# Last layer's scans: one exponential per four states, products added before TensorE sums them

## The chip, the cores and the metric

The kernel runs on one core of a Trainium2 chip. The time is the device time of one execution in microseconds. Before the change the median of three runs is 20188.83 us (20176.15 to 20194.05).

The core has five engines that run side by side, each through its own queue in order: TensorE (PE; its weight loads are listed apart as PEld), VectorE (DVE), ScalarE (ACT), GpSimd (POOL), and SyncE (SP), which here issues the DMAs. Semaphores order work between them.

## The reference, cut to what matters

Four layers in a row work on an image tensor of 8 x 48 x 48 x 96. Each is `x = x + ss2d(groupnorm(x))`. The block `ss2d` projects to 192 channels, applies a 3 x 3 depthwise convolution and a silu, and then runs four state-space scans over the 2304 pixels (by rows, by columns, and both reversed), each with 16 states per channel. A layer norm, a gate and an output projection close it.

The last layer writes its scan as cumulative sums:

```
dt = softplus(dt @ dt_proj_w + dt_proj_b)
A = -exp(A_log)
log_dA = einsum('bld,dn->bldn', dt, A)
dB_u = einsum('bld,bln->bldn', dt, B_mat) * u[..., None]
decay = exp(cumsum(log_dA, axis=1))
h = decay * cumsum(dB_u / (decay + 1e-12), axis=1)
y = einsum('bldn,bln->bld', h, C_mat)
```

The decay falls so fast along a sequence that after some pixels it is zero in float32, and `h` with it. So only a first part of each sequence can give anything.

## The kernel before, in words

The eight images are taken as four pairs. Per pair the 2 x 192 channels fill three tiles of 128 partitions: the first 128 channels of each image, and the last 64 of both together. A group is one tile (`t`), one pixel order (`ph`, rows or columns) and one direction (`d`): twelve groups per pair and layer.

In layers 0 to 2 a group is cut into `Chunk`s of 768 pixels. The last layer is handled by the class `Edge`: of each sequence only the first `EDGE` = 192 pixels are computed. A check at the very end looks whether the decay was zero there everywhere; if not, the last layer would be run again in full. In the executions here it is not run again.

An edge has 16 states, taken as four units of `QUAD` = 4 states. A unit's arrays are 128 x 4 x 192 (768 columns). For a unit:

- `load` (L930 on) has SP fetch the four rows of C, spread over the partitions, into `cb` (nine buffers).
- `decay` (L949) writes the four decays into `da` (four buffers): four ScalarE exponentials of 192 columns, each with the rate of its state as scale (L953). Its input `dl` is the running sum of delta, which `prepare` and `sum_up` (L911) have made.
- `spread` (L958) makes `rq` = 1/(decay + eps) with two activations (L960, L961) in one of three buffers of tag `bb`, and has TensorE spread the rows of B into PSUM (`b`, L678).
- `scan` (L970) multiplies on VectorE (L973, L974), runs four running sums of 192 columns into `rq` (L976), and has GpSimd multiply `cb` by the decay (L980) and by the sums (L981).
- `add_up` (L983) adds the 16 products of an edge in PSUM (`acc`, one buffer): one matmul with the identity per state (L988). `collect` then adds `acc` into `y` on VectorE (L1010).

`prepare` (L583 on) makes delta and delta x u of an edge: a small projection (L614), activations for the softplus (L622 to L628), four TensorE sums in two column halves (L634), a copy (L652) and a product (L642, L645). `dl` and `du` have two buffers.

The function `run` writes the units in program order. In step k it readies unit k+1 (`get_ready`: loads for three units ahead, decay two ahead, spread of the next), scans unit k, and sums unit k-2 (`LAG`). Beside each unit in the last layer up to ten steps of side work are issued: the prologue of the next pair (norm, projection L411 and L420, convolution L314, later projections L472) and the epilogue of the pair before (L1031 to L1140, in 16 blocks, with silu and its table loads at L270 and L271). `prepare`, prologue and epilogue share two PSUM banks (`ps`).

A planner in the framework decides when each instruction goes to its engine's queue: with priority by program order, with its own estimates of durations, and as buffers become free. `keep_order(*marks[:2])` pins the written order from the start to the last layer's first unit. In the last layer the order within the queues is thus the planner's.

Of the kernel before, what the change touches and what calls it, by code (L numbers as in the profile page):

```python
# [41 lines left out]
AF = mybir.ActivationFunctionType  # L42
ALU = mybir.AluOpType
# [6 lines left out]
P = 128  # L50
# [3 lines left out]
NS = 16  # L54
# [8 lines left out]
EDGE = 4 * W  # L63
QUAD = 4
# [39 lines left out]
def ss2d_layers_kernel(ctx: ExitStack, tc: tile.TileContext, x_in, consts, weights, out):  # L104
    nc = tc.nc
# [25 lines left out]
    ident = cst[:, 0:P]  # L131
# [54 lines left out]
    class Layer:  # L186


        def __init__(self, l):
            self.l = l  # L190
            self.rank = r = RANKS[l]
            self.nx = nx(r)
            cols, n = weight_columns(r)
            wt = wpool.tile([P, n], F32, name=f"w_{l}", tag="w")
            nc.sync.dma_start(wt, weights[l])
            part = {k: wt[:, a:b] for k, (a, b) in cols.items()}
            self.inw = part["inw"][0:DM]
            self.xp = part["xp"].rearrange("p (t f m) -> p t f m", t=2, f=2)
            self.dtw = part["dtw"].rearrange("p (k d) -> p k d", k=4)
            self.outw = part["outw"].rearrange("p (t c) -> p t c", t=2)  # L200
            self.par = part["par"].rearrange("p (t c) -> p t c", t=2)
            self.diag = None
# [56 lines left out]
    layers = {}  # L259
# [440 lines left out]
    class Chunk:  # L700
# [71 lines left out]
        def decay(self, n):  # L772

            if not self.pooled(n):
                self.exp(n, apool.tile([P, SCAN], F32, name="da", tag="da"))
# [26 lines left out]
        def scan(self, n):  # L802
            m = self.m
            way = (lambda z: z) if self.d == 0 else (lambda z: z[:, ::-1])
            carries = self.group["carry"]
            start = 0.0 if self.first else carries[:, n : n + 1]
            da, c = self.da.pop(n), self.cb[n][:, :m]
            b = self.b.pop(n)[:, :m]
            if not self.pooled(n):
                nc.vector.tensor_mul(b, self.du[n % 2], b)  # L810
            if self.l < NLAYER - 1:

                h = b if self.pooled(n) else da
                nc.vector.tensor_tensor_scan(way(h), way(da), way(b), start, ALU.mult, ALU.add)  # L814
            else:

                h = self.rq.pop(n)
                nc.vector.tensor_mul(b, h, b)
                nc.vector.tensor_tensor_scan(
                    way(h), ones.to_broadcast([P, m]), way(b), start, ALU.mult, ALU.add  # L820
                )
                nc.gpsimd.tensor_mul(c, c, da)
            nc.gpsimd.tensor_mul(c, c, h)  # L823
            if not self.last:
                end = m - 1 if self.d == 0 else 0
                late_act.append((carries[:, n : n + 1], h[:, end : end + 1]))
# [33 lines left out]
        def add_up(self, n):  # L860

            if n == 1:
                self.begin_sum()
            if n == 0:
                return
            pair = n - 1 - (n - 1) % 2
            a = n - 1 - pair
            for g in range(2):
                c = self.halves(self.cb[pair + g][:, : self.m])
                nc.tensor.matmul(  # L870
                    self.acc[64 * g : 64 * g + 64, a, : self.m // 2], twin, c[:, a, :],
                    start=False, stop=(pair + 2 == NS and not self.turns),
                )
                if a == 1:
                    del self.cb[pair + g]
            if n == NS and not self.turns:
                late_sums.append(self.collect)
# [18 lines left out]
    class Edge:  # L896


        def __init__(self, l, p, t, ph, d):
            self.l, self.p, self.t, self.ph, self.d = l, p, t, ph, d  # L900
            self.c0, self.m = 0 if d == 0 else L - EDGE, EDGE
            self.at = slice(self.c0, self.c0 + EDGE)
            self.first, self.last = ph == d == 0, ph == d == 1
            self.batches = range(2) if t == 2 else (t,)
            self.brow = self.acc = self.dts = None
            self.ready = False
            self.cb, self.da, self.rq, self.b = {}, {}, {}, {}

        def sum_up(self):
            f = self.dl[0] if self.d == 0 else self.dl[0][:, ::-1]  # L910
# [37 lines left out]

        def decay(self, i):  # L949
            self.da[i] = da = self.quad(apool.tile([P, SCAN], F32, name="da", tag="da"))  # L950
            for j in range(QUAD):
                n = (self.ph + 2 * self.d) * NS + QUAD * i + j
                nc.scalar.activation(  # L953
                    da[:, j, :], self.dl[0], AF.Exp,
                    scale=layers[self.l].a[:, int(self.t == 2), n : n + 1],
                )

        def spread(self, i):  # L958
            self.rq[i] = rq = self.quad(bbpool.tile([P, SCAN], F32, name="rq", tag="bb"))
# [9 lines left out]

        def scan(self, i):  # L970
            way = (lambda z: z) if self.d == 0 else (lambda z: z[:, ::-1])
            b, h, c = self.b.pop(i), self.rq.pop(i), self.cb[i]
            nc.vector.tensor_mul(b, self.du[0].unsqueeze(1).to_broadcast([P, QUAD, EDGE]), b)  # L973
            nc.vector.tensor_mul(b, h, b)  # L974
            for j in range(QUAD):
                nc.vector.tensor_tensor_scan(  # L976
                    way(h[:, j, :]), ones.to_broadcast([P, EDGE]), way(b[:, j, :]), 0.0,
                    ALU.mult, ALU.add,
                )
            nc.gpsimd.tensor_mul(c, c, self.da.pop(i))  # L980
            nc.gpsimd.tensor_mul(c, c, h)  # L981

        def add_up(self, i):  # L983
            if i == 0:
                self.acc = pacc.tile([P, 2 * BANK], F32, name="acc", tag="acc")
            c = self.cb.pop(i)
            for j in range(QUAD):
                nc.tensor.matmul(  # L988
                    self.acc[:, :EDGE], ident, c[:, j, :],
                    start=(i == j == 0), stop=(QUAD * i + j == NS - 1),  # L990
                )
            if QUAD * i + QUAD == NS:
                late_sums.append(self.collect)
# [430 lines left out]
```

## Time and profile before

| | |
|---|---|
| median of the runs | 20188.83 us |
| profiled execution | 20200.44 us |
| its span | 20198.6 us |
| busy: PE, DVE, ACT, POOL | 16790.8, 17667.0, 16224.6, 17769.4 us |
| last layer's units (first L953 to last L988) | 18289 to 19961 us |
| last epilogue, alone | 19963 us to the end |

A row of the profile's groups gives line, engine, operation, written and read tiles, shapes and count, then busy time in us and the mean ns of one, then the idle time of the engine just before the group, with what ended it. A 128*128 before a matmul's shapes is rows by columns of the weights; a float32 matmul shows as two records. In the table of windows, each pair of figures is an engine's busy time and its instruction count; PEclk is the share of TensorE's full clock that was granted. The chain of waits is followed back from the last instruction, at each step to what released it.

### The profile page before, as it was taken

Reading aid. Unit: us, or ns where it says so; the run is one execution under the profiler, and the core shown is the slowest. Engines: PE = TensorE matmul, PEld = TensorE weight load, DVE = VectorE, ACT = ScalarE, POOL = GpSimd, SP = SyncE. Lnnn points to the kernel's source line nnn. Section 1 sums busy time; section 2 is a strip of 40 time slices with the busy share of each in tenths; the row PEclk is TensorE's granted clock in tenths of the full one; section 3 lists DMA queues with packets and bytes.
Section 4 is the critical chain, followed back from the end, with each engine's and each line's share of the span. In section 5 each row is a group of like instructions: output and inputs, shape, how many; then the busy total and the mean of one; then the engine's idle time right before and its main releaser. Section 6 shows DMA issues by size and latency. Waiting matters only on the chain.

```text
span 20198.6 us, 314848 instructions
## 1 busy us (share of the span) xinstructions
PE 16790.8 (83%) x92962; PEld 7792.6 (39%) x92962; DVE 17667.0 (87%) x14161; ACT 16224.6 (80%) x30014; POOL 17769.4 (88%) x10121
## 2 busy tenths in 40 slices
PE   7888887887888888888887888888888887888886
PEld 3333333333333333333333333333333333334565
DVE  6999998998999999999999999999999999996553
ACT  6777887887887887887887887877877887887786
POOL 6999999999999999999999999999999999995442
PEclk9998998998998998998998999998999998999997
DMA  5888888888888888888888888888888888884221
GB/s 157 231 224 223 226 222 221 227 223 220 225 226 224 224 231 224 223 228 223 225 228 223 223 225 226 223 226 221 221 224 222 222 225 221 220 222 117 79 74 50
DMA packets 2021150, 4200.80 MB, mean 208 GB/s; under 512 B 375920, under 2 KB 789360, under 8 KB 2017904
## 3 DMA queue, kind: packets, MB, share of 16 engines
q1 hardware_dynamic: 2019440, 4180.55, 79.2%
q8 instruction: 762, 12.48, 0.3%
q14 instruction: 948, 7.77, 0.2%
HBM read 4026.64 MB, written 152.27 MB: 207 GB/s over the span
## 4 chain that ended last, share of the span: by engine, by line
PE 21%; ACT 17%; DVE 14%; DMA 10%; issue 9%; POOL 3%; SPq 2%; DVEq 0%; POOLq 0%; ACTq 0%
DVE da L814 7%; PE acc L870 5%; PE ps L634 4%; DMA bb<-xd 4%; DVE b L810 4%; DMA cb<-xd 4%; ACT b L780 3%; ACT dl L589 3%; PE ps L314 2%; PE b L678 2%; ACT du L589 2%; POOL cb L823 2%; DVE bb L814 2%; ACT da L780 2%; SPq L740 1%
## 5 line engine op out<-in xcount | busy, mean ns | idle before, releaser
L823 POOL TENSOR_TENSOR cb<-cb,da 128x768 f32<-128x768 f32 x4320 | 7835.9, 1819 | 749.3 <-issue 253.1
L870 PE MATMUL acc<-cb,twin 128*64 128x384 f32 x27648 | 7200.8, 539 | 721.3 <-POOL cb L823 704.5
L814 DVE TENSOR_TENSOR_SCAN da<-da,carry,b 128x768 f32<-128x768 f32 x2880 | 5223.2, 1814 | 176.0 <-DVE b L810 0.9
L757 POOL TENSOR_TENSOR bb<-bb,du 128x768 f32<-128x768 f32 x2592 | 4716.9, 1820 | 222.2 <-DMA bb<-xd 125.6
L823 POOL TENSOR_TENSOR cb<-cb,bb 128x768 f32<-128x768 f32 x2592 | 4706.8, 1816 | 100.2 <-DVE bb L814 50.7
L810 DVE TENSOR_TENSOR b<-du,b 128x768 f32<-128x768 f32 x4320 | 4085.6, 946 | 690.2 <-PE b L678 604.2
L678 PE MATMUL b<-brow,pick 96*64 96x512 bf16 (+2 forms) x18816 | 2852.5, 353 | 1886.2 <-DVE da L814 1528.4
L780 ACT ACTIVATE da<-dl,a 128x768 f32<-128x768 f32 x4320 | 4011.3, 930 | 213.5 <-POOL cb L823 183.0
L870 PEld LDWEIGHTS acc<-cb,twin 128*64 128x64 f32 x27648 | 2452.5, 149 | 2998.4 <-POOL cb L823 1333.5
L814 DVE TENSOR_TENSOR_SCAN bb<-b,carry,bb 128x768 f32<-128x768 f32 x1728 | 3109.6, 1800 | 106.0 <-ACT b L780 35.6
L780 ACT ACTIVATE b<-dl,a 128x768 f32<-128x768 f32 x2592 | 2335.3, 901 | 623.2 <-DVE da L814 598.4
L678 PEld LDWEIGHTS <-pick 96*64 96x64 bf16 x18816 | 1077.9, 115 | 4164.4 <-DVE da L814 2717.6
L814 DVE TENSOR_TENSOR_SCAN da<-da,b 128x768 f32<-128x768 f32 x1440 | 2525.3, 1754 | 87.4 <-DVE b L810 1.4
L314 PE MATMUL ps<-pad,diag 128*64 128x480 f32 (+1 forms) x8640 | 2339.7, 567 | 34.6 <-ACT du L589 24.4
L589 ACT COPY dl<-ps 64x384 f32<-64x384 f32 x3456 | 1632.6, 472 | 697.9 <-PE ps L634 659.6
L589 ACT COPY du<-ps 64x384 f32<-64x384 f32 x3456 | 1633.5, 473 | 200.7 <-DVE ps L645 109.8
L634 PE MATMUL ps<-du,cst 128*64 128x384 f32 (+1 forms) x7296 | 1704.5, 506 | 76.5 <-ACT du L628 65.6
L814 DVE TENSOR_TENSOR_SCAN bb<-b,bb 128x768 f32<-128x768 f32 x864 | 1502.1, 1739 | 145.5 <-ACT b L780 92.2
L634 PE MATMUL ps<-dl,cst 128*64 128x384 f32 (+1 forms) x7296 | 1485.2, 483 | 0.0
L614 PE MATMUL ps<-dts,w 6*128 6x384 f32 (+5 forms) x2432 | 961.4, 605 | 205.0 <-DMA dts<-xd 105.4
L622 ACT ACTIVATE du<-ps,w 128x384 f32<-128x384 f32 (+1 forms) x912 | 519.9, 570 | 714.6 <-PE ps L614 701.0
L314 PEld LDWEIGHTS ps<-pad,diag 128*64 128x64 f32 x8640 | 751.8, 139 | 885.0 <-issue 729.6
(144 smaller groups left out, 19166.4 us busy)
## 6 DMA issues: line engine op xcount, KB each, us to landing
cb<-xd SPq DMA_DIRECT2D x13952, 192.0 KB
bb<-xd SPq DMA_DIRECT2D x5184, 192.0 KB
brow<-xb SPq DMA_DIRECT2D x864, 72.0 KB
ey<-yd SPq DMA_DIRECT2D x256, 216.0 KB
cb<-xd SPq DMA_DIRECT2D x128, 384.0 KB
yd<-y SPq DMA_DIRECT2D x216, 192.0 KB
ex<-xs SPq DMA_DIRECT2D x256, 108.0 KB
xb<-parts SPq DMA_DIRECT2D x96, 216.0 KB
```

Of the source, the lines that this page charges most:

```text
L314: nc.tensor.matmul(ps[half, :m], ly.diag[:, int(t == 2), j, half], pad[:, r0 + dy : r0 + dy + nr, dx : dx + W], start=(j == 0), stop=(j == 8),
L589: nc.scalar.copy(z[64 * h : 64 * h + 64, g, at], v[64 * g : 64 * g + 64])
L614: nc.tensor.matmul(o[:, :m], ly.dtw[q0 : q0 + r, k, chans], dts[q0 : q0 + r, at], start=True, stop=True,)
L622: nc.scalar.activation(e, v, AF.Abs, bias=bias)
L634: nc.tensor.matmul(v[half], ident[:, half], z1, start=(i == 0), stop=(i == 3))
L678: nc.tensor.matmul(o[64 * h : 64 * h + 64], pick[:, b, n : n + 1].to_broadcast([2 * NR, 64]), rows, start=True, stop=True,)
L757: nc.gpsimd.tensor_mul(b, b, self.du[n % 2])
L780: nc.scalar.activation(da, self.dl[n % 2], AF.Exp, scale=layers[self.l].a2[:, int(self.t == 2), n % 2, k, i : i + 1],)
L810: nc.vector.tensor_mul(b, self.du[n % 2], b)
L814: nc.vector.tensor_tensor_scan(way(h), way(da), way(b), start, ALU.mult, ALU.add)
L823: nc.gpsimd.tensor_mul(c, c, h)
L870: nc.tensor.matmul(self.acc[64 * g : 64 * g + 64, a, : self.m // 2], twin, c[:, a, :], start=False, stop=(pair + 2 == NS and not self.turns),)
```

## The change

Three edits, all in `Edge`:

1. `decay`: one GpSimd product of `dl` (repeated for four states) and the four rates (repeated over 192 pixels) into `da`, then one ScalarE exponential of all 768 columns in place. The four scaled exponentials go.
2. `scan`: the tile `rq`, which holds the running sums, is kept in `self.h` for later.
3. `add_up`: VectorE adds the four products of the unit over the states (`tensor_reduce` over a rearranged view with a step of 192 columns) into the first 192 columns of the kept `rq` tile, and TensorE adds this one array into `acc`, in two matmuls of 64 columns of the identity instead of four of 128.

```diff
         def decay(self, i):
             self.da[i] = da = self.quad(apool.tile([P, SCAN], F32, name="da", tag="da"))
-            for j in range(QUAD):
-                n = (self.ph + 2 * self.d) * NS + QUAD * i + j
-                nc.scalar.activation(
-                    da[:, j, :], self.dl[0], AF.Exp,
-                    scale=layers[self.l].a[:, int(self.t == 2), n : n + 1],
-                )
+            n = (self.ph + 2 * self.d) * NS + QUAD * i
+            a = layers[self.l].a[:, int(self.t == 2), n : n + QUAD]
+            nc.gpsimd.tensor_mul(
+                da, self.dl[0].unsqueeze(1).to_broadcast([P, QUAD, EDGE]),
+                a.unsqueeze(2).to_broadcast([P, QUAD, EDGE]),
+            )
+            nc.scalar.activation(da, da, AF.Exp)
...
         def scan(self, i):
             way = (lambda z: z) if self.d == 0 else (lambda z: z[:, ::-1])
-            b, h, c = self.b.pop(i), self.rq.pop(i), self.cb[i]
+            b, c = self.b.pop(i), self.cb[i]
+            self.h[i] = h = self.rq.pop(i)
...
         def add_up(self, i):
             if i == 0:
                 self.acc = pacc.tile([P, 2 * BANK], F32, name="acc", tag="acc")
-            c = self.cb.pop(i)
-            for j in range(QUAD):
+            c, z = self.cb.pop(i), self.h.pop(i)[:, 0, :]
+            nc.vector.tensor_reduce(
+                z, c.rearrange("p n m -> p m n"), mybir.AxisListType.X, ALU.add
+            )
+            for g in range(2):
+                half = slice(64 * g, 64 * g + 64)
                 nc.tensor.matmul(
-                    self.acc[:, :EDGE], ident, c[:, j, :],
-                    start=(i == j == 0), stop=(QUAD * i + j == NS - 1),
+                    self.acc[half, :EDGE], ident[:, half], z,
+                    start=(i == 0), stop=(QUAD * i + QUAD == NS),
                 )
```

More of the change, by code (lines that the diff above doesn't have):

```diff
@@ L906, in __init__ @@
             self.ready = False
-            self.cb, self.da, self.rq, self.b = {}, {}, {}, {}
+            self.cb, self.da, self.rq, self.b, self.h = {}, {}, {}, {}, {}
         def sum_up(self):
```

## The prediction

> **What bounds the kernel now.** I first read the page's 40 slices, to find where the changed code runs, because it runs in the last layer only.
>
> ```profile
> PE   7888887887888888888887888888888887888886
> PEld 3333333333333333333333333333333333334565
> DVE  6999998998999999999999999999999999996553
> ACT  6777887887887887887887887877877887887786
> POOL 6999999999999999999999999999999999995442
> ```
>
> For 36 slices GpSimd and VectorE are full; in the last four they fall to about half while TensorE and ScalarE stay at 8. The first quad product (L980) starts at 18,300 us and the last (L981) at 19,955: a stage of 1,673 us from the first exponential, 12 edges x 4 units for each of four pairs, 192 units of 8.7 us. From 19,963 only the last epilogue runs (235 us, without these lines); before 18,290 nothing changes. Next, the engines' busy time in windows cut at the pairs' first units, and then at the end of the third epilogue:
>
> ```profile
> core 0: us, PE busy (x) PEld busy (x) DVE busy (x) ACT busy (x) POOL busy (x), PEclk, DMA share, GB/s
> 18300.00:18723.00 423.00, 372.25 (x2490) 237.03 (x2490) 223.13 (x384) 338.12 (x637) 178.34 (x111) 0.95 0.31 88
> 18723.00:19153.00 430.00, 379.79 (x2653) 252.83 (x2654) 223.94 (x381) 340.51 (x641) 178.05 (x111) 0.93 0.27 77
> 19153.00:19579.00 426.00, 379.00 (x2662) 251.50 (x2660) 221.15 (x375) 340.34 (x641) 177.77 (x107) 0.93 0.27 75
> 19579.00:19824.00 245.00, 184.62 (x1416) 153.59 (x1412) 114.74 (x197) 196.03 (x359) 85.91 (x48) 0.86 0.26 71
> 19824.00:19963.00 139.00, 93.19 (x552) 71.87 (x552) 94.88 (x168) 96.23 (x195) 85.76 (x48) 0.76 0.22 65
> ```
>
> In three pairs PE is busy 0.88 to 0.89, ACT 0.80, DVE 0.52, POOL 0.42. The fourth pair has no prologue to carry. Its first 245 us hold an epilogue of 16 blocks, which alone takes 235 us, so that stretch is paced by the epilogue's own chain. Its last 139 us have no side work: about 25 units at 5 to 6 us. Then the groups of the stage, kept apart by shape:
>
> ```profile
> L976 DVE TENSOR_TENSOR_SCAN rq<-ones,b 128x192 f32<-128x192 f32 x768 | 364.9, 534 | 12.7
> L988 PE MATMUL acc<-cb,cst 128*128 128x192 f32 x1536 | 352.7, 372 | 72.3 <-POOL cb L981 64.2 <-DVE y L1010 6.4 <-ACT y L887 1.3
> L981 POOL TENSOR_TENSOR cb<-cb,rq 128x768 f32<-128x768 f32 x192 | 347.9, 1812 | 499.6 <-DVE rq L976 456.5 <-PE ps L411 17.8 <-ACT eo L1140 8.1
> L980 POOL TENSOR_TENSOR cb<-cb,da 128x768 f32<-128x768 f32 x192 | 347.1, 1813 | 417.2 <-ACT da L953 399.2 <-PE acc L988 10.1 <-PE ps L314 6.1
> L953 ACT ACTIVATE da<-dl,a 128x192 f32<-128x192 f32 x767 | 293.5, 443 | 29.5 <-DVE dl L911 29.0
> ```
>
> The sum's matmuls are the largest TensorE group, and GpSimd's idle 917 us in front of its two products is waiting, not work. Last, the chain of waits in the stage:
>
> ```profile
> by line: PE ps L314 17.6%; PE acc L988 11.0%; DVE rq L976 4.9%; POOL cb L981 4.5%; issue 4.5%; ACT da L953 3.7%; PE ps L1031 3.2%; PE ps L634 2.8%; PE ps L1032 2.6%; PE b L678 2.4%; PE ps L1135 2.1%; POOL cb L980 2.1%; ACT L270 2.1%; PE ps
> ```
>
> Summed by engine, PE holds 928 of 1,673 us of it and ACT 340. So TensorE's in-order queue is the nearest bound, fed through ScalarE; the change takes work from both.
>
> **What the Trainium skill says.** "ScalarE: Activation LUTs", What ACT_TABLE_LOAD costs: 186 ns + 0.833 N, and some 93 ns for each pointer operand. For 192 columns with a pointer scale that is 439 ns, for 768 without one 826; the trace has 440 (L953) and 834 (L961). "GPSIMD Engine Reference", Performance versus the Vector engine: two inputs cost about 2.6 cycles an element, estimated 1,664 ns for 768 before dispatch; the trace has 1,812. "VectorE: DVE Perf Modes", perf-mode tier table: tensor_reduce runs at one element per cycle only. The trace agrees: L231 reads 128 elements in 262 ns, L154 reads 48, strided, in 202. "TensorE: Matmul & The Clock Gate", Part 1: idle gaps lower the clock. The windows agree: 0.95 granted at 0.88 busy, 0.76 at 0.67.
>
> **The change, part by part, per unit.**
>
> ScalarE loses four exponentials. They occupy 292.9 us for 758, overlaps counted once: 1.55 us per unit. It gains one like L961, 0.83. Saved: 0.71 us, 136 us over 192 units.
>
> TensorE loses four 128-column products of 192 columns, eight records: 352.7/192 = 1.84 us. It gains two 64-column halves, four records. The nearest row is L634 (128*64, 128x192, 752 records busy 86.3 us: 0.115 each), so 0.46. Saved: 1.38 us, 265 us in all. Even at L988's 0.23 a record it would be 0.92, still half.
>
> GpSimd gains one product of 768 with two broadcast inputs. No row has a stride-0 input; L980, L981 and L757 give 1.81, which I take. Below, were a repeated operand free of the read port, a single-input loop would be an estimated 1 us by the same page; above, half more (2.7) by its pitfalls table, which names long strides that are absent here. Per pair POOL goes from 178 to 265 us of some 410: room. In the last 139 us it goes from 86 to some 130: no room.
>
> VectorE gains a reduce of 768 to 192. From L231's slope and offset (128/0.96 + 135 ns) it is 0.935; taken 0.95. Its step of 768 bytes has no row here, so the upper end is twice that. DVE per pair: 223 to 269 us.
>
> New waits: an exponential now waits for GpSimd, whose queue holds the product behind L980 and L981 of earlier units, L981 being the one that waits for scans (456 us). Whoever waits for that exponential (L960, L980) waits along. The reduce stands in VectorE's queue behind a POOL result; behind it stand the next L973, L974 and scans. DMA loads and SP's order do not change; the cb buffers come free sooner, after the reduce, at no gain since no large wait names them.
>
> The costliest new hold is the buffer. The reduce writes into rq, of which there are three. Before, rq was free when L981 ended; now it is held to the end of the matmuls. Taking the n-th instruction of each line as unit n, rq's first activation to L981's end is 13.0 us on average, to the end of L988 22.9; three buffers at 8.7 us a unit allow 26.1. It fits on average; in the convolution quarters, where L988 runs up to 17 us after L981, it is at the limit.
>
> **The sum on the chain.** L988: 11.0% of 1,673 = 184 us, scaled 0.46/1.84, is 46: -138. L953: 3.7% = 62, 40 units, at 0.83 is 33: -29. Where the chain comes to that exponential from delta's running sum (25 waits on L911), the GpSimd product is put between: +45. L981's 75 us are 41 visits, each followed by a reduce: +41. That is -81. Clock: other TensorE work on the chain, 928 - 294 - 184 = 450 us, loses some 4% as PE empties: +20. The last 25 units, at POOL's limit: +13. So -48 with the order as it is. The order is planned anew, though: were the three pairs as full of TensorE work as now (0.89), each would be (372 - 66)/0.89 = 344 us instead of 425, some -240 in all. I take a fifth of the way between, since two PSUM banks for all side work and the epilogue's own chain stay: -48 - 38 = -86. The profiled execution took 20,200.4 us (span 20,198.6, 1.8 around it), so 20,114; the runs' median stands 11.6 below it, so about 20,103 there.
>
> **Rivals.** First, a denser plan: TensorE's 265 us are mostly given back, 19,930 to 20,040 us. For it: PE at 0.89. Against: much of the chain is epilogue and convolution, untouched. Second, no gain: GpSimd's product and the reduce, in series between delta and the sum, cost what the matmuls give, 20,148 to 20,230. For it: the last 25 units already run at 5 to 6 us, and each needs 5.4 us of POOL. Third, slower: the rq ring. If L988 goes on 13 us behind L981 in the convolution quarters, a unit's hold is 14.3 (activation to L981) + 4 (GpSimd's fuller queue) + 1.2 (reduce) + 13 + 0.6 = 33 us; a third is 11 us against 9.8, over some 108 units +140, to 20,330. It decides once the hold passes three times the present period. Against it: L988 lags because TensorE is overfull, which the change relieves. That the change does not act is excluded: L953, L980 and L988 are its lines and run 192 units.
>
> **How the numbers follow.** My forecast, 20,040 to 20,148: 0.48, and within it 20,103. Denser plan 0.20, no gain 0.13, ring 0.19. A change under 0.2% (40 us) can't be told from none here: faster 0.68, same 0.13, slower 0.19. From 19,970 (a third of the dense case below) to 20,250 (most of the ring above) holds eight in ten; the unknown costs of product and reduce, at their upper ends 0.9 us each on the 25 and 41 chain visits (+59), lie inside.
>
> **What would show it.** Right: L988 with 768 records of 64 columns near 90 us; one exponential per unit of 0.83; a GpSimd row at 1.81; a reduce at 0.95; pairs one to three near 400 us, PE at 0.76; the last stretch a little longer. Wrong: ACT's first rq activation waiting for TensorE's sum (the ring), a reduce far over 1 us, L973 idle behind the reduce, or PE still above 0.85.

## The result, and the profile after

The change makes the kernel slower: 20396.8 us median (20382.12 to 20410.47), against 20194.05 (20176.15 to 20211.87) for the kernel before on the same chip. The ratio is 1.0102, with a 95% interval of 1.0088 to 1.0116. One thousandth of the time is 20.2 us; all ratios below are turned into us with that, so this one is +206. Every kernel was compared with runs of the kernel before on its own chip.

In the profiled execution the span is 20380.3 us. The last epilogue alone takes 237 us (235 before). The whole difference lies in the 192 units of the last layer: from the start of their first scan to the end of their last, 1,862 us against 1,656, so +206. (What stands ahead of the first scan was 22 us shorter in this execution, so the two spans differ by only 182.) These are the page's 40 slices after the change:

```profile
PE   7887887887888888888888888888888888877775
PEld 3333333333333433433433333433433433334444
DVE  6999999999999999999999999999999999996553
ACT  6777887887887878887878878878878878876665
POOL 6999999999999999999999999999999999995543
```

TensorE and ScalarE have dropped from 8 to 7 and 6 in the last slices, as the change meant them to. VectorE and GpSimd have not risen to full. No engine has become so busy that its load alone would explain the loss, and yet the time is longer. Next, the engines' busy time in windows cut at the pairs' first units, at the end of the third epilogue and at the last unit:

```profile
core 0: us, PE busy (x) PEld busy (x) DVE busy (x) ACT busy (x) POOL busy (x), PEclk, DMA share, GB/s
18285.00:18773.00 488.00, 365.66 (x2286) 221.72 (x2286) 288.62 (x434) 321.64 (x506) 247.54 (x160) 0.80 0.25 74
18773.00:19252.00 479.00, 369.10 (x2474) 227.18 (x2476) 288.32 (x436) 320.57 (x503) 246.81 (x159) 0.81 0.23 69
19252.00:19719.00 467.00, 362.30 (x2464) 225.68 (x2464) 282.15 (x421) 318.25 (x497) 244.78 (x154) 0.83 0.24 69
19719.00:20000.00 281.00, 181.27 (x1385) 146.62 (x1384) 145.98 (x219) 198.80 (x307) 120.81 (x74) 0.77 0.21 62
20000.00:20143.00 143.00, 54.89 (x369) 29.86 (x370) 123.49 (x181) 69.00 (x102) 106.68 (x64) 0.54 0.17 53
```

The pairs take 488, 479, 467 and 424 us, against 423, 430, 426 and 384. TensorE is busy 0.75 of the first pair, ScalarE 0.66, VectorE 0.59, GpSimd 0.51. The loss is spread over all four pairs; the last stretch, where GpSimd was to be tight, adds only some 4 us of it. The granted clock fell from 0.95 to about 0.81. The groups of the stage, kept apart by shape:

```profile
L978 DVE TENSOR_TENSOR_SCAN rq<-ones,b 128x192 f32<-128x192 f32 x764 | 362.0, 533 | 3.3
L994 PE MATMUL acc<-rq,cst 128*64 128x192 f32 x768 | 142.1, 410 | 157.9 <-DVE rq L989 150.2 <-ACT da L957 4.2 <-DVE y L1016 1.9
L983 POOL TENSOR_TENSOR cb<-cb,rq 128x768 f32<-128x768 f32 x192 | 347.9, 1813 | 479.7 <-DVE rq L978 402.6 <-ACT rq L961 20.8 <-ACT eo L1146 8.5
L982 POOL TENSOR_TENSOR cb<-cb,da 128x768 f32<-128x768 f32 x192 | 345.3, 1814 | 79.4 <-ACT da L957 79.1
L957 ACT ACTIVATE da<-da 128x768 f32<-128x768 f32 x188 | 157.3, 838 | 136.6 <-POOL da L953 136.1
L953 POOL TENSOR_TENSOR da<-dl,a 128x768 f32<-128x768 f32 x188 | 270.7, 1465 | 292.9 <-DVE dl L911 278.2 <-DMA cb<-xd 10.9 <-ACT rq L961 2.1
L989 DVE TENSOR_REDUCE rq<-cb 128x192 f32<-128x768 f32 x192 | 285.7, 1488 | 241.4 <-POOL cb L983 241.0 <-DMA brow<-xb 0.2
```

The work that left is gone: the sum's matmuls are busy 142 us instead of 353, the exponentials 157 instead of 294. The three new instructions have something in common: each is preceded by a long idle time of its own engine, and each names another engine as what ended it. The waits of the stage put that beside each other (engine, line and what it waited for: us in total, times, longest us). Of the kernel before:

```profile
POOL cb L980 <- ACT da L953: 399.2, 100, 27.8
DVE b L974 <- ACT rq L961: 173.0, 63, 10.1
PE acc L988 <- POOL cb L981: 64.2, 54, 2.7
ACT da L953 <- DVE dl L911: 29.0, 25, 3.1
```

And of the changed kernel:

```profile
POOL da L953 <- DVE dl L911: 278.2, 37, 31.6
DVE rq L989 <- POOL cb L983: 233.9, 128, 7.7
DVE b L976 <- ACT rq L962: 147.3, 64, 7.8
PE acc L994 <- DVE rq L989: 143.6, 72, 4.8
ACT da L957 <- POOL da L953: 136.1, 91, 6.0
ACT rq L961 <- PE acc L994: 36.7, 22, 3.9
```

Three waits are new and large: VectorE for GpSimd's products (234 us), GpSimd for delta's running sum (278), ScalarE for GpSimd's new product (136). The last line, the `rq` ring of the third rival, is small. The chain of waits in the stage:

```profile
by line: issue 10.1%; PE ps L314 6.7%; POOL cb L983 6.4%; DVE rq L978 5.3%; POOL cb L982 4.8%; POOL da L953 4.7%; DVE rq L989 3.1%; DVE b L976 2.2%; PE ps L1141 1.8%; PE ps L1037 1.7%; PE ps L1142 1.6%; PE ps L1140 1.5%; PE ps L1038 1.3%; A
```

The sum's matmuls have left its first places, and so has most of TensorE: 397 of 1,853 us (18,290 to 20,143), where it was 928 of 1,673. GpSimd (297) and VectorE (254) have taken its place.

### The profile page after: what moved, and what is told of

It is laid out like the page before. It is cut to its first block, busy times and chain, and to the rows that moved or that the text cites. A ratio compares the mean times of both kernels' runs of the same rounds, so it can differ in the third digit from the quotient of the medians.

```text
span 20380.3 us, 313007 instructions
## 1 busy us (share of the span) xinstructions
PE 16716.7 (82%) x92194; PEld 7667.9 (38%) x92194; DVE 17921.1 (88%) x14353; ACT 16147.2 (79%) x29458; POOL 18041.2 (89%) x10313
## 5 line engine op out<-in xcount | busy, mean ns | idle before, releaser
L314 PE MATMUL ps<-pad,diag 128*64 128x480 f32 (+1 forms) x8640 | 2334.9, 569 | 41.3 <-ACT du L589 24.7
L314 PEld LDWEIGHTS ps<-pad,diag 128*64 128x64 f32 x8640 | 756.6, 140 | 896.2 <-issue 732.1
```

The lines of the kernel that those rows point to most:

```text
L314: nc.tensor.matmul(ps[half, :m], ly.diag[:, int(t == 2), j, half], pad[:, r0 + dy : r0 + dy + nr, dx : dx + W], start=(j == 0), stop=(j == 8),
```

## The experiments

The theory after the result: TensorE and ScalarE were busy and on the chain, but no bound, so the work taken from them is worth nothing; the two new hand-overs, GpSimd to VectorE and VectorE to GpSimd to ScalarE, hold the heads of in-order queues, and that costs the 206 us. The rivals were the `rq` ring, the strided reduce (longer than forecast) and the lower clock. As a second measure beside the ratios: in every run's profile, the stretch from the first scan of the stage to the last differs from the kernel before's by the same amount within 25 us.

### The two halves apart

e1 has edit 1 alone (product on GpSimd, one exponential; `scan` and `add_up` as before):

```diff
-            for j in range(QUAD):
...
-                nc.scalar.activation(
...
+            nc.gpsimd.tensor_mul(
+                da, self.dl[0].unsqueeze(1).to_broadcast([P, QUAD, EDGE]),
+                a.unsqueeze(2).to_broadcast([P, QUAD, EDGE]),
+            )
+            nc.scalar.activation(da, da, AF.Exp)
```

> Only the first edit: one GpSimd product and one exponential per unit; the four matmuls per unit stay. In-order theory (the product stands at the head of GpSimd's queue until delta's running sum is there, and the two products of earlier units stand behind it): slower than before by 60 to 150 us, with some 250 us of GpSimd idle before the new product. Ring theory (the kept rq buffer costs the time): no loss, 0 to -60 us, since rq is free again after the second product. Reduce theory (1.49 us where 0.95 was forecast, on VectorE): no loss either.

Measured: 1.0059 (1.0042 to 1.0076), +119 us, as the theory had it. e2 has edits 2 and 3 alone (the four exponentials stay):

```diff
+            self.h[i] = h = self.rq.pop(i)
...
+            nc.vector.tensor_reduce(
+                z, c.rearrange("p n m -> p m n"), mybir.AxisListType.X, ALU.add
+            )
+            for g in range(2):
+                half = slice(64 * g, 64 * g + 64)
...
+                    self.acc[half, :EDGE], ident[:, half], z,
```

> Only the other two edits: VectorE adds the four products into the kept rq tile, TensorE sums one array; the four scaled exponentials stay. In-order theory: VectorE still waits at the reduce for GpSimd's product, but GpSimd is lighter; between -60 and +60 us of before. Ring theory: the whole loss is here, +150 to +220 us. Reduce theory: some +50 to +100 us.

Measured: 1.0072 (1.0055 to 1.0089), +145 us. That is outside what the theory expected (at most +60) and just under what the ring expected, so the ring had to be tested next, and the weight of VectorE's wait was underrated. Each half loses by itself; together they would be +264, the changed kernel has +206.

### The rivals of ring, reduce and clock

e3 is the changed kernel with a tile of its own for the sum, so that `rq` is free at the end of L983 as before:

```diff
+    zpool = ctx.enter_context(tc.tile_pool(name="z", bufs=3))
...
-            c, z = self.cb.pop(i), self.h.pop(i)[:, 0, :]
+            c, z = self.cb.pop(i), zpool.tile([P, EDGE], F32, name="z", tag="z")
```

> The changed kernel, but the reduce writes into a small tile of its own (three buffers), so rq is free as before once GpSimd's second product has read it. Ring theory: 100 us or more of the loss come back, 20,300 or less. In-order theory: under 50 us come back, most of it in the convolution quarters. Reduce theory: nothing comes back.

Measured: 1.0101 (1.0084 to 1.0118), +204 us, as the changed kernel. The ring is not it. e4 replaces the strided reduce by two contiguous additions:

```diff
-            nc.vector.tensor_reduce(
-                z, c.rearrange("p n m -> p m n"), mybir.AxisListType.X, ALU.add
-            )
+            nc.vector.tensor_add(c[:, :2, :], c[:, :2, :], c[:, 2:, :])
+            nc.vector.tensor_add(z, c[:, 0, :], c[:, 1, :])
```

> The changed kernel, with the strided reduce replaced by two contiguous adds (384 columns, then 192, the second into the kept rq tile); by the 768-column products at 0.955 us they should take about 0.55 and 0.35 us, 0.9 in place of 1.49. Reduce theory: 0.6 us x 192 = 110 us at most come back, at least 60. In-order theory: 20 to 60 us come back, as far as VectorE's queue is on the path. Ring theory: under 30 us.

Measured: 1.0120 (1.0103 to 1.0137), +242 us: not faster (that it is slower than the changed kernel is not clear of the intervals). It doesn't test the reduce's length, though, since the two additions took longer than the reduce, 1.08 and 0.63 us on average against 1.49 (the last section says why); e7 below tests it. e8 is the changed kernel with three matmuls per unit whose output nobody reads, to keep TensorE's clock up:

```diff
+            for _ in range(3):
+                nc.tensor.matmul(
+                    self.acc[:, BANK : BANK + EDGE], ident, cst[:, 0:EDGE], start=True, stop=True
                 )
```

> The changed kernel with three idle identity matmuls of 192 constant columns per unit, beside the two halves, into an unused part of the sum's PSUM tile: TensorE's work per unit is as before the change, the clock should be too. Clock theory: faster than the changed kernel in spite of more work, by 50 us or more (20,345 or less), clock back at 0.90 or above in the first three pairs. Queue theory: slower than the changed kernel, by 0 to 100 us, whatever the clock.

Measured: 1.0115 (1.0098 to 1.0132), +232 us. From 18,300 to 19,500 us the clock rose from 0.82 to 0.87, not to the 0.90 or more that was expected, and the time did not fall. So e8 speaks against the clock as the cause of the loss, but only over part of the clock's fall, and with more matmuls to run.

### Relief without the new instructions

What would TensorE's saving be worth if nothing came for it? e5 is the kernel before with one identity matmul per unit instead of four; three of four states are left out of the sum.

```diff
-            for j in range(QUAD):
+            for j in range(1):
...
-                    start=(i == j == 0), stop=(QUAD * i + j == NS - 1),
+                    start=(i == 0), stop=(QUAD * i + QUAD == NS),
```

> The kernel before, with one identity matmul per unit in place of four: TensorE does 1.38 us less per unit and nothing is added anywhere. It leaves three of four states out of the sum. If TensorE's work bounds the stage, as the prediction had it: 20,100 or less, at least 90 us faster than before. Clock theory (less TensorE work lowers the granted clock, and all its other work pays): between -30 and +60 us of before, with the clock of the first three pairs near 0.82 in place of 0.94. Queue theory (only the added waits cost): faster by 50 us or more at any clock.

Measured: 1.0006 (0.9999 to 1.0013). The engines' busy time from 18,300 to 19,500 us, columns as in the windows above; first the kernel before:

```profile
18300.00:19500.00 1200.00, 1063.77 (x7308) 690.14 (x7308) 632.58 (x1077) 954.88 (x1793) 506.58 (x307) 0.94 0.28 78
```

Then with one matmul per unit:

```profile
18300.00:19500.00 1200.00, 973.45 (x6252) 585.28 (x6249) 638.38 (x1064) 937.66 (x1757) 529.75 (x321) 0.84 0.30 85
```

In this execution the stage begins 51 us later (first scan at 18,350 us, 18,299 before). In 1,200 us from the first scan on, TensorE has 6,403 records instead of 7,303 and is busy 990 us instead of 1,063, at a clock of 0.85. It stands idle more, and the kernel takes the time that it took. So the saving, together with the lower clock that came with it, is worth nothing. The expectation of the queue theory, 50 us faster at any clock, was missed; that of the clock theory was met.

Could the clock have eaten a real gain? TensorE's other matmuls took 6% longer on average in the stage (in the windows above, L314 went from 567 to 580 ns, L1135 from 263 to 299). On the chain's other 745 us of TensorE work that makes an estimated 45 us, a third of the 138 that the prediction had for the relief. And in the chain of e5 (18,350 to 20,026 us) that other work takes 726 us: it didn't grow. L988 fell from 183 to 47 us there, as forecast; ScalarE took 43 us more than before, GpSimd 47, issue 44 and DMAs 15. So the place that the matmuls left went to other engines, and not to slower matmuls.

e6 does the same for ScalarE: one exponential per unit straight from `dl`, at the first state's rate (the other three rates are left out), and no GpSimd product.

```diff
+            nc.scalar.activation(
+                da, self.dl[0].unsqueeze(1).to_broadcast([P, QUAD, EDGE]), AF.Exp,
+                scale=layers[self.l].a[:, int(self.t == 2), n : n + 1])
```

> The kernel before, with one exponential of 768 columns per unit in place of four of 192, all four states with the rate of the first (so the decays of three states are wrong), and no GpSimd product. ScalarE does 0.71 us less per unit. If ScalarE feeds the chain: 20 to 100 us faster. If the stage is bound by waits of other engines: within 30 us of before. With it the cost of the GpSimd product alone is the run of the first edit alone (20,323) less this one: 120 us or more by the queue theory, 60 or less by the clock theory.

Measured: 1.0000 (0.9993 to 1.0007). ScalarE's exponentials are busy 175 us instead of 294, and nothing comes of it, at a clock that stayed at 0.93. With that, e1's 119 us belong to the GpSimd product and what waits for it.

### The wait or the instruction

e7 is e2 with the reduce over VectorE's own running sums (into its own tile) instead of GpSimd's products; the factors C and decay are left out of the sum, though GpSimd still multiplies. The instruction stays, its wait for GpSimd goes; TensorE's sum doesn't wait for GpSimd any more either.

```diff
-            c, z = self.cb.pop(i), self.h.pop(i)[:, 0, :]
+            h, z = self.h.pop(i), zpool.tile([P, EDGE], F32, name="z", tag="z")
+            self.cb.pop(i)
...
-                z, c.rearrange("p n m -> p m n"), mybir.AxisListType.X, ALU.add
+                z, h.rearrange("p n m -> p m n"), mybir.AxisListType.X, ALU.add
```

> The second and third edit alone (20,356), but the reduce reads VectorE's own running sums, not GpSimd's product, and writes a small tile of its own: it costs the same and waits for GpSimd no more. The factor C and the decay are left out of what is summed. Queue theory (VectorE stands at the reduce for GpSimd): 100 us or more faster than with the wait, about 20,250 or less. Clock theory: under 60 us faster, clock still near 0.82.

Measured: 1.0003 (0.9996 to 1.0009), +6 us. e9 keeps what is computed: e2 with its own tile, and an order edge on VectorE that puts the reduce of unit i behind the scans that were written last, those of unit i+2. By then GpSimd is through with unit i.

```diff
+                newest["scan"] = nc.vector.tensor_tensor_scan(
...
+                ).ins
...
+            with tc.issue_after(newest["scan"]):
+                nc.vector.tensor_reduce(
+                    z, c.rearrange("p n m -> p m n"), mybir.AxisListType.X, ALU.add
+                )
```

> The second and third edit alone (20,356), all that they compute kept, but the reduce of a unit has its place in VectorE's queue behind the scans of the unit two later, and a small tile of its own. If the loss is VectorE standing at the head of its queue for GpSimd, with the epilogue's and prepare's products behind it: within 50 us of before, some 100 us faster than without the new place. If the loss is the longer way from GpSimd's product to TensorE's sum: no faster than 20,330, since that way grows.

Measured: 1.0021 (1.0012 to 1.0029), +42 us. The reduce in the groups of the three kernels, first e2:

```profile
L988 DVE TENSOR_REDUCE rq<-cb 128x192 f32<-128x768 f32 x192 | 285.3, 1486 | 209.9 <-POOL cb L982 209.1
```

then over VectorE's own sums:

```profile
L990 DVE TENSOR_REDUCE z<-rq 128x192 f32<-128x768 f32 x192 | 287.8, 1503 | 3.3
```

and ordered late:

```profile
L992 DVE TENSOR_REDUCE z<-cb 128x192 f32<-128x768 f32 x192 | 284.7, 1484 | 0.0
```

The busy time is the same 285 us in all three. The idle time ahead of it goes from 210 to 3 and to 0, and the loss from 145 to 6 and to 42 us. Without its wait, a reduce of 1.49 us per unit is free (e7); one that stands waiting at the head of VectorE's queue costs more. With every value computed, its new place in the queue alone gives back 103 us (e9); with the sum free of GpSimd too, 139 (e7). The lower clock alone doesn't make the loss: in 1,200 us from the first scan on it is 0.82 in e2, 0.85 in e9 and 0.86 in e7, which loses nothing. What e9 still loses may be the longer way from GpSimd's product to the sum, which its expectation named; no run shows it.

The product has its own pair. e10 is e1 with the product on VectorE, which makes delta's running sum itself, so that no wait between the two is left:

```diff
-            nc.gpsimd.tensor_mul(
+            nc.vector.tensor_mul(
```

> The first edit alone (20,323), but the product of delta with the rates is made by VectorE, where delta's running sum was made, not by GpSimd. If GpSimd's queue makes the loss (its own products late, and ScalarE standing at the exponential for it): within 40 us of before. If it is the extra step between delta and the exponential: 20,280 or more.

Measured: 1.0031 (1.0019 to 1.0043), +63 us: about half of e1's 119 come back. The result lies between the two expectations, so it doesn't put the whole loss on GpSimd's queue. The waits of e1:

```profile
POOL da L953 <- DVE dl L911: 262.0, 40, 27.5
ACT rq L961 <- POOL cb L982: 135.6, 39, 7.2
ACT da L957 <- POOL da L953: 83.2, 58, 6.8
```

and of e10:

```profile
ACT rq L961 <- POOL cb L982: 108.6, 44, 6.0
ACT da L957 <- DVE da L953: 46.7, 23, 2.8
```

GpSimd's wait for delta is gone, and ScalarE's for the product has halved. e11 is the changed kernel with both remedies:

```diff
-            nc.gpsimd.tensor_mul(
+            nc.vector.tensor_mul(
...
+            with tc.issue_after(newest["scan"]):
+                nc.vector.tensor_reduce(
```

> The whole change with both waits moved: the product on VectorE, the reduce behind the scans of the unit two later, in its own tile. If the two waits at queue heads are the whole loss: within 50 us of before, some 150 us faster than the changed kernel. If the added instructions themselves count (VectorE has 2.4 us more per unit than before): 20,300 or more.

Measured: 1.0049 (1.0032 to 1.0065), +99 us. That is about e9's 42 and e10's 63 together: what each remedy leaves adds up. So the two waits are not the whole loss; about half of the 206 us stays when both are moved, and the expectation that it met is that of the added instructions. VectorE has the reduce and the product in addition, and holds 575 of 1,766 us of the chain (182 of 1,673 before). A chain's share is no proof, as e5 showed; the instructions themselves remain a candidate.

### What sets the pace of the stage

If neither relief helps, what sets the 8.7 us of a unit? Four kernels change only how many side steps are issued beside a unit; the first three are the kernel before, e15 is e9.

```diff
-                for _ in range(10 if l in short else 0 if ends else 1):
+                for _ in range(14 if l in short else 0 if ends else 1):
```

With 14 (e12):

> The kernel before with up to 14 steps of side work written beside each unit of the last layer in place of 10; nothing else differs. If the chain of side work through the two PSUM banks sets the pace of the stage, its length is what it was: within 60 us of before, with shorter periods at the end of each pair and longer ones ahead of it. If the units' own chain sets the pace, delaying units behind side work costs 100 us or more.

With 8 and 6 (e13, e14):

> The kernel before with up to 8 side steps between two units of the last stage instead of 10. If the units' own chain sets the pace of the stage, as the run with 14 steps suggests (+127 us), fewer side steps bring it forward: 20,150 us or less. If the pace is that of the side chain (the epilogue and the preparation of the next pair), it comes later: 20,260 us or more. If 10 is a balance of the two, within 30 us of the kernel before.

> The kernel before with up to 6 side steps between two units. Units' chain: 20,150 us or less, and not above the run with 8. Side chain: 20,300 us or more, since a pair's side steps no longer fit between its 48 units and are issued in a block at the pair's end. Balance: slower than the run with 8, by 50 us or more.

With 8 and the late sum (e15):

> Edits 2 and 3 alone with the sum ordered two units later (the late sum, 20,253 us), and up to 8 side steps between two units instead of 10. If the 40 us that the late sum still loses are units held back behind side work, 20,210 us or less, and below the kernel before if the run with 8 steps is. If they are the side chain's own lateness, 20,290 us or more.

Measured, from 14 to 6: 1.0065 (1.0047 to 1.0083), 1.0032 (1.0020 to 1.0045) and 1.0073 (1.0056 to 1.0090), so +131 at 14, +65 at 8 and +147 us at 6, around nothing at 10. e15: 1.0057 (1.0040 to 1.0073), +115, about e9's 42 and e13's 65 together. Ten is the best of the four: with more steps or fewer the stage grows. e13 lost more than its expectation of a balance allowed (30 us), and e15's loss is the one expected of late side work. This fits a balance of units and side work, in a stage limited by two interleaved orders of waiting, rather than by an engine's work, but it doesn't name the wait.

The last three have the next edge's delta forced at an edge's first unit instead of its second: the kernel before (e16), the changed kernel (e17) and e11 (e18).

```diff
-            if n == max(0, per - 1 - DECAYS):
+            if n == max(0, per - 1 - DECAYS - (l in short)):
```

> The kernel before, with the next edge's delta forced at the edge's first unit instead of its second. If the first exponential of an edge is held by a late delta in the kernel before too, 20 to 80 us faster; if the present order is a balance like that of the side steps, the same or up to 60 us slower.

> The changed kernel, with the next edge's delta forced one unit earlier. If the product on GpSimd loses its 106 to 120 us because it waits for a late delta at the head of the queue, most of that comes back beyond what the kernel before gains: 20,300 us or less, and GpSimd's 278 us of waiting for delta's sum fall below 100. If it is the place in the queue, 20,370 us or more.

> The version with the product on VectorE and the sum two units later (some 20,290 us beside this kernel before), with the next edge's delta forced one unit earlier. Late delta: the 56 us of the product go, 20,230 us or less. Place in the queue: 20,270 us or more.

Measured: e16 0.9977 (0.9967 to 0.9986), −46 us; e17 1.0082 (1.0065 to 1.0099), +166; e18 1.0045 (1.0029 to 1.0062), +91. e16 is faster than both kernels, by the one line above. In the same window as before:

```profile
18300.00:19500.00 1200.00, 1095.29 (x7556) 702.69 (x7557) 643.44 (x1106) 976.49 (x1848) 517.73 (x316) 0.95 0.28 81
```

TensorE is busy 0.91 there, about 30 us more than in the kernel before: the queue that I had taken for the bound had room. The changed kernel gains some 40 us by the same line (the intervals overlap), so the change costs about the same on either base. On late delta the runs decide nothing: GpSimd's wait for its sum in e17 is still 264.7 us in 42 waits, and ScalarE's in e16 is 30.3 us in 28 waits (29.0 in 25 before), so delta came no earlier for those who wait for it. Why e16 is faster stays open.

## Why the prediction was wrong

The forecast was 20,103 us, faster; the result is slower and above the range. Step by step:

**TensorE's queue as the nearest bound.** This is the step that failed. The chain gave TensorE 928 of 1,673 us, and L988 184 of them; I turned that share into a saving of 138. e5 took away three of the four matmuls and nothing else: +12 us, interval −2 to +26. The exponentials' share, −29, is 0 ± 14 by e6. A chain names what came last at each step. When that came sooner, something else that was almost as late took its place: L988's part of the chain did fall to 47 us (forecast 46), but ScalarE, GpSimd, issue and DMAs together took 149 us more, at no gain at all.

**The new waits.** The prediction named both: an exponential behind GpSimd's queue, and a reduce at the head of VectorE's with the next unit's products and scans behind it. It priced them by visits: 25 of one product (+45), 41 of one reduce (+41). Measured, the product costs about 119 (e1 less e6) and the wait of the reduce about 139 (e2 less e7). Charging the instruction's own length per visit was the error. For the reduce that is shown: the instruction is free (e7), and what is lost is what stands behind it while it waits. For the product it is shown in part: without its wait for GpSimd it still costs 63 (e10). The timeline shows one such place in the changed kernel; columns are start, length, the instruction, and in brackets the idle time before it. VectorE:

```profile
18644.97 1.43 DVE L978 TENSOR_TENSOR_SCAN rq<-ones,b 128x192 f32<-128x192 f32 x3
18650.69 1.51 DVE L989 TENSOR_REDUCE rq<-cb 128x192 f32<-128x768 f32 x1 [4.29 <-POOL cb L983]
18652.13 1.81 DVE L975 TENSOR_TENSOR b<-du,b 128x768 f32<-128x768 f32 x2
```

and GpSimd at the same time:

```profile
18644.58 4.32 POOL L953 TENSOR_TENSOR da<-dl,a 128x768 f32<-128x768 f32 x3 [3.65 <-DVE dl L911]
18648.85 1.81 POOL L983 TENSOR_TENSOR cb<-cb,rq 128x768 f32<-128x768 f32 x1
18650.62 3.59 POOL L982 TENSOR_TENSOR cb<-cb,da 128x768 f32<-128x768 f32 x2
```

GpSimd waits 3.65 us for a delta, then runs three of the new products one behind another; the product L983 starts the moment they are through. The reduce waits 4.29 us for that L983, and two products of the next units, which need nothing of GpSimd, follow it without a gap. Here one edit's wait feeds the other's. Over the stage the reduce is preceded by 241 us of idle time with both edits, and by 210 in e2.

**Durations.** GpSimd's product: 1.465 us, forecast 1.81, inside the bounds of 1 and 2.7. The exponential: 0.838, forecast 0.83. The sum's matmuls: 142 us, forecast about 90; the saving was 211 instead of 265. The reduce: 1.49 us, forecast 0.95, inside its upper end of 1.9. I had it from the Trainium skill, "VectorE: DVE Perf Modes", perf-mode tier table (one element per cycle) and from two short rows; here, with a step of 768 bytes between the elements, it takes half as long again, though no run takes the step apart from the instruction. Of the prediction's signs of being wrong this one came true, a reduce far over 1 us, but by e7 it isn't the cause.

**Pairs and clock.** 400 us a pair was forecast, 478 measured. PE at 0.76 was right (0.75 to 0.78 in three pairs), but by luck: TensorE was busy 366 us a pair where 306 were forecast, and the pair was longer by about the same fifth. The clock fell by 14%; the prediction had TensorE's other work lose 4%, and in the working charged it to 450 us, leaving out L314's 294 without a reason. By e5, e7 and e8 it isn't what costs most. The last stretch grew by 4 us instead of 13.

**The fifth of the way to a denser plan (−38).** Nothing of it came; in e5, with TensorE relieved and no new wait, the plan didn't close up either.

**Slips in the working.** Four things in it are not as written, and none decides. 41 reduces of 0.95 are 39 us, not 41. The 25 waits for delta are all of ScalarE's in the stage, not those counted on the chain. L231 is a single row of 128 elements, which gives no slope, and 262 ns less the 133 of that formula leaves 129, not 135. And the ring's 108 units at 1.2 us make 130 us, not 140.

**The rivals.** "No gain" named the right place, product and reduce in series between delta and the sum, and was too low: it let the matmuls give something back, and it, too, priced the new instructions by their length. The slower rival had the right side and the wrong mechanism: ScalarE waits 36.7 us for the ring, and e3 frees it for nothing.

The sum as measured: TensorE's relief 0, ScalarE's 0, the product +119, the reduce's wait +139, together +258; both at once give +206, so part of the two seems to overlap. Open is what makes the remaining 99 us of e11, the added instructions or another wait, and which wait sets the 8.7 us.

## What to carry to other kernels

An engine that is 0.88 busy and leads the chain of waits need not be the bound: take its work away for one run, leaving out a part of the result if need be, before anything is added in exchange. When an operation is moved to another engine, price the place where it waits, with all that stands behind it in that queue, and not its length; if its result is not needed soon, order it behind work of its own engine that is ready (here the loss went from 145 to 42 us). How side work is interleaved with the main loop, and where the next step's preparation is written, can be worth more than an engine's load (here −46 us for one line).

## What the runs showed that was not expected

**Two inputs in SBUF on VectorE collide with GpSimd.** Why did two contiguous additions take longer than the strided reduce? Their durations (min, median, max in ns), in e4:

```profile
L989 DVE TENSOR_TENSOR cb<-cb x192: 486/559/7253, 18324.0 to 20202.3; 128x384 f32<-128x384 f32 x192
```

and of the product on VectorE in e10:

```profile
L953 DVE TENSOR_TENSOR da<-dl,a x192: 886/951/5694, 18273.1 to 19975.1; 128x768 f32<-128x768 f32 x192
```

Sorted by whether a GpSimd record runs at the same time: of 192 additions, 104 without one take 0.555 us on average and 0.564 at most, 88 with one take 1.70 on average. The product takes 0.948 without (84) and 1.60 with (108). The reduce, with one input, takes 1.484 and 1.492. The Trainium skill says this in "SBUF — State Buffer", Who interferes with whom: a VectorE instruction with two SBUF inputs contends with GpSimd's reads, a `tensor_reduce` never does; the trace agrees. In e10 it adds 0.37 us on average (1.32 less 0.95) to a product that ScalarE waits for. That this is a part of the 63 us that e10 loses is argued, not shown.

**GpSimd is faster with repeated inputs.** The product of two broadcast operands (L953) takes 1.465 us, those of two full ones (L982, L983) 1.81, for the same 768 columns. The full ones also write in place, and no run takes the two apart.

**TensorE stays busy as it empties.** In e5 it has 12% fewer records in 1,200 us from the first scan on (6,403 against 7,303), and its busy time fell by 7% only, while the granted clock went from 0.94 to 0.85 and its other matmuls took 6% longer. The busy share of an engine with such a clock understates how much was taken from it.
